# Band softmax sums split by key halves, band groups normalized in other steps, and other issue orders in a transformer layer on one core

## The chip, the cores and the metric

The kernel runs on one core of a Trainium2 chip. The metric is device time in microseconds (us) of one execution; the time before is the median of three runs. The names of the profile are used: PE is TensorE's matrix products, PEld its weight loads, DVE VectorE, ACT ScalarE, POOL GpSimd, SP SyncE, which issues most of the DMAs.

## The reference

One transformer layer on x of shape (2, 256, 128, 128), that is batch, time T, bands FB, channels C, in float32. Three residual blocks follow each other:

```
xt = LN(x);  x = x + MHA(xt over T,  4 heads, causal mask)
xf = LN(x);  x = x + MHA(xf over FB, 4 heads, mask |i - j| <= 16)
xn = LN(x);  x = x + (gelu(xn @ w1.T + b1) @ w2.T + b2)      # inner width 512
```

MHA is softmax(q k^T / sqrt(32) + mask) v with input and output projections. The attention over bands works on 128 positions, and each query sees the keys at most 16 positions away.

## The kernel before, in words

**Groups and runs.** The work is cut into groups of four tiles of 128 positions by 128 channels (512 columns). 128 groups of attention over time (`OverTime`) come first. Then come 16 runs; a run is 8 groups of attention over bands (`OverBands`, here "band groups", numbered 0 to 7) and then the 8 groups of the feed-forward block (`FeedForward`) on the same data. The first of the 16 runs overlaps the end of the attention over time.

**Steps.** `BoundedPath.run` (L1275 on) writes out the order of everything by hand. Step n of its loop works on several groups at once: the scores, exponentials and masks of group n, the weighing of group n-1, the output product of group n-2, queries, keys and values of group n+1, the fetch of the normalized input of group n+2, the normalization of group n+3, and statistics further ahead. Each engine runs its instructions in the order in which they are written (`InOrder`, L897 to L909, pins them; for this reason nearly every instruction of the profile carries line L907). An instruction that has to wait therefore holds up everything behind it on its engine.

**Products.** `product` (L646) makes a product of 128 by 128 by N as four, one for each strip of 32 output partitions, so that four tiles of the array of 128 rows by 32 columns (`128*32` in the profile) work side by side. The scores use tiles of 32 by 64 (`32*64`), eight side by side. Every float32 product shows as two instructions.

**One step of a band group, n.** On PE, in this order: the scores of n (L775; heads 0 to 3, for each tile two halves of 64 keys by 80 queries); the sums of the softmax weights of n-1 (L814, the product of ones with the weights p, `128*32`, 512 columns a head, into the bank `rp`); the weights times the values (into `op`); the output product of n-2 (L630); queries and keys of n+1 (L571), then values (L590). On ACT: four exponentials of the scores, Ln and Exp that invert the sums of n-1 (L602), the copies of queries, keys and values. On POOL: the band masks of heads 0 to 2, two instructions each (L800); head 3 is masked on DVE ahead of its exponential (L790). On DVE: the mask of head 3, the normalization and the 32 by 32 transposes of group n+3 (L441 and L458), the add of the output product of n-2 (L636), then the division for n-1 (L615: rp times r0, then u, then oT), then in some steps the statistics of a feed-forward group (L1302). The transposed tiles go through DRAM: `turn` writes them with four DMAs, `fetch` reads them one step later.

**Roots.** The reciprocal root of a group's variance is taken on POOL (`root`). For the first three feed-forward groups of a run the statistics are written in band steps 3, 4 and 5, behind the division, and the root at the head of steps 4, 5 and 6, ahead of that step's masks in POOL's order.

**A feed-forward step.** On PE: the first two of four hidden blocks of n (L841), the second product of n-1 (L869, four column tiles, four accumulated parts each), the last two hidden blocks of n. On ACT: GELUs, two and two. On DVE: normalization of n+3, the add of the second product (L886), statistics. After each second add four DMAs on SP store the result.

**Banks.** PSUM has eight banks of 512 columns. Outside the attention over time they were handed out in turn (L943), whoever asked next.

Of the kernel before, what the change touches and what calls it, by code (L numbers as in the profile page):

```python
# [19 lines left out]
P = 128  # L20
H = 4
D = 32
# [12 lines left out]
LARGE = 1e20  # L35
EXP_SET = "natural_log_exp_and_others"
# [327 lines left out]

def by_tile(t):

    return t.rearrange("p (i t q) -> p i t q", i=NT, q=D)


class Group:  # L370
# [7 lines left out]
    def __init__(self, path, src, dst, before=None, store=None):  # L378
        self.path, self.src, self.dst = path, src, dst
        self.before, self.store = before, store  # L380

# [76 lines left out]
    def turn(self):  # L458
# [3 lines left out]
        z = path.work.tile([P, H, P], F32, name="z", bufs=2)  # L462
# [98 lines left out]
class Attention(Group):  # L561
    which = None
    swapped = ()
# [7 lines left out]
    def queries_keys(self):  # L571
        path = self.path
        wf = path.k.wf[self.which]
        self.qp = path.bank([P, NT * P], "qp", self.place.get("qp", path.held.pop("qp", None)))
        product(path, self.qp, wf[:, 0:P], self.xnT)

        self.kp = path.bank([P, NT * P], "kp", self.place.get("kp"))
        product(path, self.kp, wf[:, P : 2 * P], self.xnT)

    def take_query(self):  # L580
        path = self.path
        self.qT = path.work.tile([P, NT * P], F32, name="qT")
        path.scalar.activation(self.qT, self.qp, AF.Identity, bias=path.k.bq[self.which], scale=1.0)

    def take_key(self):
        path = self.path
        self.kT = path.work.tile([P, NT * P], F32, name="kT")
        path.scalar.copy(self.kT, self.kp)

    def values(self):  # L590
        path = self.path
        wv = path.k.wf[self.which][:, 2 * P : 3 * P]
        self.vp = path.bank([P, NT, P], "vp", self.place.get("vp"))
# [3 lines left out]
    def take_values(self):  # L597
        path = self.path
        self.v = path.work.tile([P, NT, P], F32, name="v", bufs=4)
        path.scalar.copy(self.v, self.vp)  # L600

# [13 lines left out]
    def divide(self):  # L615

        path, vector = self.path, self.path.vector
        if self.r0 is None:
# [3 lines left out]
            vector.tensor_scalar(self.oT, u, -1.0, None, ALU.mult)  # L622
            return
        vector.tensor_tensor(self.rp, self.rp, self.r0, ALU.mult)
# [3 lines left out]
        vector.tensor_tensor(by_rows(self.oT), by_tile(self.op), by_tile(u), ALU.mult)  # L628

    def output(self):  # L630
        path = self.path
        self.yp = path.bank([P, NT, P], "yp", self.place.get("yp", path.held.pop("yp", None)))
# [3 lines left out]
    def finish(self):  # L636
        self.path.vector.tensor_tensor(self.dst(), self.yp, self.dst(), ALU.add)
        if self.store is not None:
            self.store()
# [13 lines left out]
class OverTime(Attention):  # L653
# [7 lines left out]
    def values(self):  # L661
        path = self.path
        wv = path.k.wf[self.which][:, 2 * P : 3 * P]
        self.vp = [path.bank([P, 2, P], "vp", self.place.get(f"vp{s}")) for s in range(2)]
# [5 lines left out]
    def take_values(self):  # L670
        path = self.path
        self.v = path.work.tile([P, NT, P], F32, name="v", bufs=4)
        for s in range(2):
            path.scalar.copy(self.v[:, 2 * s : 2 * s + 2], self.vp[s])

    def first_tiles(self):
# [3 lines left out]
        self.s0 = {h: path.bank([P, 2, 2 * P], "sp", path.banks[f"a{h}"]) for h in range(H)}  # L680

    def second_tiles(self):
# [3 lines left out]
        self.s1 = {h: path.bank([P, 2, P], "sp", path.banks[f"b{h}"]) for h in range(H)}  # L686
# [15 lines left out]
    def first_weights(self, heads):  # L702
        for h in heads:
            self.path.scalar.activation(self.p0[:, :, h], self.s0[h], AF.Exp)

    def second_weights(self, heads):
        for h in heads:
            self.path.scalar.activation(self.p1[:, :, h, 0], self.s1[h], AF.Exp)

# [17 lines left out]
    def weigh(self):  # L727
        path, v = self.path, self.v
        rp = path.bank([P, 2, 2, P], "rp", self.place.get("rp"))
# [4 lines left out]
        op = path.bank([P, 2, 2 * P], "op", self.place.get("op"))  # L734
# [33 lines left out]
class OverBands(Attention):  # L768
# [3 lines left out]
    follow = ("yp",)  # L772
    by_vector = 1

    def scores(self, heads):  # L775
        path = self.path
        self.sp = {h: path.bank([P, NT * P], "sp") for h in heads}
# [12 lines left out]
    def first_function(self):  # L790
# [6 lines left out]
        for h in range(H):  # L797
            path.scalar.activation(self.p[:, h].rearrange("p i q -> p (i q)"), self.sp[h], AF.Exp)

# [13 lines left out]

    def weigh(self):  # L814
        path = self.path

        path.held = {name: path.turn_of_bank() for name in self.follow}
        self.rp = path.bank([P, NT * P], "rp")
        for h in range(H):
            path.tensor.matmul(  # L820
                self.rp[rows_of(h), :], path.k.ones[:, 0:D], self.p[:, h].rearrange("p i q -> p (i q)"),
                start=True, stop=True,
            )
        self.op = path.bank([P, NT * P], "op")
# [7 lines left out]
class FeedForward(Group):  # L832
    last = False
# [679 lines left out]
```

## Time and profile before

| | |
|---|---|
| timed runs | 2631.95, 2633.58 and 2634.81 us, median 2633.58 |
| span of the profiled execution | 2631.9 us, granted TensorE clock 1.000 |
| attention over time | up to about 920 us of the span |
| 16 runs of band and feed-forward groups | the rest, some 106 us each |
| DVE, ACT, POOL busy | 81%, 70%, 74% of the span |
| HBM read and written | 167.98 MB and 166.72 MB |

The profiled execution has a span of its own, from its first to its last instruction; the timed runs also hold what lies around it. Times in rows of a timeline are from the start of the span. A row of the timeline gives start, duration, engine, line, operation, output<-inputs, shapes and how many instructions were merged; in brackets the idle time of the engine ahead of it and what ended that. A row of a group gives busy time and the mean of one in ns, then idle time and who ended it.

### The profile page before, as it was taken

The page shows a single profiled execution, that of the slowest core. Times are in us where ns is not written, and L with a number is a line of the kernel's source. Part 1 is how long each engine was busy: PE and PEld are TensorE (multiplying, and loading weights), DVE is VectorE, ACT ScalarE, POOL GpSimd, SP SyncE. Part 2 cuts the span into 40 slices and gives each one's busy share as a digit, 9 for nine tenths or more (in the row PEclk, how much of TensorE's full clock was granted, in tenths as well). Part 3 has the DMA queues.
Part 4 walks back from the last instruction along what each step waited for, and adds up shares of the span by engine and source line. Part 5 has one row for each costly group of instructions (what it writes and reads, how often), then busy time and mean ns, then how long its engine had stood idle before and what let it go on. Part 6 is the DMA issues. An engine that isn't in the chain of part 4 may idle for free.

```text
span 2631.9 us, 156460 instructions
## 1 busy us (share of the span) xinstructions
PE 2617.8 (99%) x68688; PEld 1837.4 (70%) x68688; DVE 2140.8 (81%) x6410; ACT 1838.8 (70%) x3543; POOL 1958.6 (74%) x2311
## 2 busy tenths in 40 slices
PE   9999999999999999999999999999999999999999
PEld 6666666666766767666777776667676677777776
DVE  8888888888888887977878779788797797887974
ACT  7989988999899875564655746647557466475573
POOL 7999999999999987666667666665776666757762
PEclk9999999999999999999999999999999999999999
DMA  6656555565565454445454544554454445554543
GB/s 155 167 149 158 149 149 149 155 155 149 149 158 149 122 127 119 115 123 127 118 124 124 123 122 117 126 128 120 122 126 120 120 119 131 123 120 123 123 104 88
DMA packets 469797, 344.97 MB, mean 131 GB/s; under 512 B 43120, under 2 KB 404464, under 8 KB 469104
## 3 DMA queue, kind: packets, MB, share of 16 engines
q1 hardware_dynamic: 468408, 334.41, 50.5%
q8 instruction: 540, 8.85, 1.5%
q14 instruction: 153, 1.25, 0.2%
q10 hardware_dynamic: 696, 0.46, 0.1%
HBM read 167.98 MB, written 166.72 MB: 127 GB/s over the span
## 4 chain that ended last, share of the span: by engine, by line
PE 99%; DVE 0%; issue 0%; DMA 0%; ACT 0%; ACTq 0%; DVEq 0%
PE bank L907 99%; DMA x<-in_x 0%; DVE xh L907 0%; DVE bank L907 0%; DVE res L907 0%; DVE stats L907 0%; DVE oT L907 0%; DVE u L907 0%; DVE xnT L907 0%; ACTq L907 0%; ACT p L907 0%; DVE vy L907 0%; ACT lnv L907 0%; DVE mv L907 0%; ACT root L907 0%
## 5 line engine op out<-in xcount | busy, mean ns | idle before, releaser
L907 ACT ACTIVATE hT<-bank,b 128x512 f32<-128x512 f32 x512 | 348.1, 688 | 524.2 <-PE bank L907 483.2
L907 POOL TENSOR_SCALAR_AFFINE_SELECT pf<-pf 128x512 f32<-128x512 f32 x768 | 477.7, 637 | 185.3 <-ACT pf L907 159.1
L907 PEld LDWEIGHTS bank<-w2T_sb,hT 128*32 128x32 f32 x16384 | 467.4, 110 | 54.8 <-issue 29.0
L907 PE MATMUL bank<-xnT,wf 128*32 128x512 f32 x4096 | 492.4, 592 | 0.5 <-DVE xnT L907 0.5
L907 PE MATMUL bank<-xnT,w1f 128*32 128x512 f32 x4096 | 486.3, 592 | 0.2 <-issue 0.2
L907 PE MATMUL bank<-w2T_sb,hT 128*32 128x128 f32 x16384 | 482.8, 273 | 1.0 <-issue 1.0
L907 ACT ACTIVATE p<-bank 128x512 f32<-128x512 f32 (+1 forms) x1024 | 430.6, 494 | 62.9 <-PE bank L907 62.9
L907 DVE TENSOR_SCALAR xh<-x,mv,rstd 128x160 f32<-128x160 f32 (+1 forms) x1012 | 394.3, 432 | 59.7 <-POOL rstd L907 49.4
L907 POOL TENSOR_SCALAR_AFFINE_SELECT p<-p 128x1024 f32<-128x1024 f32 (+2 forms) x384 | 364.5, 949 | 57.5 <-ACT p L907 49.1
L907 PEld LDWEIGHTS bank<-wf,xnT 128*32 128x32 f32 x8192 | 243.3, 110 | 144.1 <-issue 101.6
L907 POOL TENSOR_TENSOR p<-p,p 128x512 f32<-128x512 f32 x256 | 324.6, 1291 | 10.6
L907 DVE BATCH_NORM_STATS2 stats<-x 128x6 f32<-128x128 f32 x1536 | 329.0, 276 | 3.4 <-DMA x<-in_x 3.4
L907 POOL TENSOR_SCALAR rstd<-mv 128x4 f32<-128x4 f32 x251 | 57.8, 230 | 361.7 <-DVE mv L907 360.5
L907 PEld LDWEIGHTS bank<-xnT,w1f 128*32 128x32 f32 x4096 | 183.6, 110 | 171.6 <-issue 109.6
L907 PE MATMUL bank<-qT,kT 32*64 32x80 f32 (+4 forms) x16384 | 302.0, 271 | 0.1
L907 PEld LDWEIGHTS bank<-qT,kT 32*64 32x64 f32 x16384 | 260.0, 131 | 51.2 <-ACT kT L907 50.6
L907 DVE TENSOR_TENSOR res<-bank,res 128x512 f32<-128x512 f32 (+1 forms) x259 | 170.3, 658 | 153.3 <-PE bank L907 144.7
L907 ACT ACTIVATE pf<-bank 128x512 f32<-128x512 f32 x512 | 265.8, 602 | 35.5 <-PE bank L907 31.3
L907 PE MATMUL bank<-wn,oT 128*32 128x128 f32 x8192 | 283.8, 274 | 0.1
L907 DVE STREAM_TRANSPOSE z<-xh 128x512 f32<-128x512 f32 x380 | 270.3, 711 | 13.3
L907 PE MATMUL bank<-wf,xnT 128*32 128x128 f32 x8192 | 276.5, 273 | 0.0
L907 POOL TENSOR_TENSOR rstd<-rstd,mhalf 128x4 f32<-128x4 f32 x251 | 260.8, 1039 | 20.9
(100 smaller groups left out, 3820.3 us busy)
## 6 DMA issues: line engine op xcount, KB each, us to landing
turned<-z SPq DMA_DIRECT2D x1520, 64.0 KB, 2.7
xnT<-turned SPq DMA_DIRECT2D x380, 256.0 KB, 3.2
x<-res SPq DMA_DIRECT2D x256, 128.0 KB, 2.5
x<-x SPq DMA_DIRECT2D x128, 256.0 KB, 4.1
out<-res SPq DMA_DIRECT2D x252, 128.0 KB, 2.3
x<-in_x SPq DMA_DIRECT2D x124, 256.0 KB, 4.3
x<-in_x SPq DMA_DIRECT2D x4, 128.0 KB, 2.8
x<-in_x SPq DMA_DIRECT2D x6, 64.0 KB, 2.9
```

Of the source, the lines that this page charges most:

```text
L907: return self.tc.keep_in_program_order(emit(*args, **kwargs))
```

## The change

Four things are changed in the runs; the attention over time keeps its order.

1. *Sums in two parts*, for band groups 0 to 6 of each run (those whose next group is a band group too). The queries 0 to 47 of a tile see only the keys 0 to 63, and the queries 80 to 127 only the keys 64 to 127. Their sums are products over 64 keys, one half into `rp`, the other into a bank of its own, `lower`; the 32 queries in the middle are summed over 128 keys. The outer sums come directly behind the scores. Ln and the multiplication by r0 are made in two parts each.
2. *Orders in band steps.* The queries of n+1 are computed (and their copy queued) between the outer and the middle sums, ahead of the output product; keys and values stay where they were.
3. *Orders in feed-forward steps.* The second product of n-1 is split after two column tiles, with the third hidden block of n between the halves. The stores are put one step later, from ScalarE's queue in feed-forward steps.
4. *Normalization ahead.* When group n+3 is a band group (not of the first run), band group n+6 is normalized and turned in the same step. So groups 3 to 7 are done three steps earlier: groups 3, 4 and 5 in the last three feed-forward steps of the run before, 6 and 7 in band steps 0 and 1, and band steps 2, 3 and 4 normalize nothing. The tiles in DRAM get 8 buffers for 3, z gets 3 for 2.

Banks are now taken from a list of free ones in the order in which their last readers were written.

```diff
+EDGE = HALF - BAND
...
+    def outer_sums(self):
+
+        self.split = True
+        self.rp = self.take("rp", [P, NT * P])
+        self.lower = self.take("lower", [P, NT * EDGE])
+        for h in range(H):
+            self.sums_of(h, in_tiles(self.rp)[:, :, 0:EDGE], slice(0, EDGE), slice(0, HALF))
+            self.sums_of(h, in_tiles(self.lower), slice(P - EDGE, P), slice(HALF, P))
+
+    def middle_sums(self):
+        q = slice(EDGE, P - EDGE)
+        for h in range(H):
+            self.sums_of(h, in_tiles(self.rp)[:, :, q], q, slice(0, P))
+
+    def sums_of(self, h, to, q, rows):
+        self.path.tensor.matmul(
+            to[rows_of(h)], self.path.k.ones[rows, 0:D], self.p[rows, h, :, q],
+            start=True, stop=True, skip_group_check=True,
+        )
+
+    def invert(self):
...
+        path.scalar.activation(in_tiles(ln)[:, :, 0 : P - EDGE], in_tiles(self.rp)[:, :, 0 : P - EDGE], AF.Ln)
+        path.scalar.activation(in_tiles(ln)[:, :, P - EDGE : P], in_tiles(self.lower), AF.Ln)
+        self.r0 = path.work.tile([P, NT * P], F32, name="r0", bufs=2)
+        path.scalar.activation(self.r0, ln, AF.Exp, scale=-1.0)
+
+    def multiply(self):
...
+        vector.tensor_tensor(rp[:, :, low], in_tiles(self.lower), r0[:, :, low], ALU.mult)
+        self.give("lower")
+        vector.tensor_tensor(rp[:, :, q], rp[:, :, q], r0[:, :, q], ALU.mult)
...
     def weigh(self):
         path = self.path
 
-        path.held = {name: path.turn_of_bank() for name in self.follow}
-        self.rp = path.bank([P, NT * P], "rp")
-        for h in range(H):
...
+        if self.split:
+            self.middle_sums()
+        else:
+            self.rp = self.take("rp", [P, NT * P])
...
-        self.op = path.bank([P, NT * P], "op")
+        self.op = self.take("op", [P, NT * P])
...
+    def weigh_around(self, other):
+
+        self.zp = self.take("zp", [P, NT, P])
+        self.weigh_tiles(range(0, 2))
+        other.hidden((2,))
+        self.weigh_tiles(range(2, NT))
+        other.hidden((3,))
...
+        def turn_ahead(n):
+            for i in (n + 3, n + 6):
+                ahead = at(n + 3, OverBands) and at(i, OverBands) and i not in run0
+                if not at(i, OverTime) and (i == n + 3 or ahead) and not at_turn(i):
+                    do(i, "normalize", "turn")
...
+            self.storing = self.scalar if feeds[2] and n < len(groups) - NT else self.sync
+            do_at(n - 2, FeedForward, "put")
...
-            do_at(n + 3, (OverBands, FeedForward), "normalize", "turn")
+            turn_ahead(n)
...
-            do(n - 1, "weigh")
+            if bands[1] and bands[2]:
+                do(n - 1, "outer_sums")
+            if bands[2] and bands[3]:
+                do(n + 1, "queries")
+            if feeds[1] and feeds[2]:
+                groups[n - 1].weigh_around(groups[n])
+            else:
+                do(n - 1, "weigh")
             do(n - 1, "invert_exactly" if turn else "invert")
+            if bands[2] and bands[3]:
+                do(n + 1, "take_query")
...
             if bands[2] or turn:
                 do(n - 2, "output", "finish")
...
             do(n - 1, "divide")
...
             if bands[2] or turn:
                 statistics_of_feed(n)
-            if not turn:
+            if feeds[1] and feeds[2]:
+                do(n, "second_function")
+            elif not turn:
                 do(n, "second_half", "second_function")
...
-            do_at(n + 1, OverBands, "queries_keys", "take_query", "take_key")
+            if bands[2] and bands[3]:
+                do(n + 1, "keys", "take_key")
+            else:
+                do_at(n + 1, OverBands, "queries_keys", "take_query", "take_key")
```

In the code `bands[i]` and `feeds[i]` say whether group n-2+i is a band group or a feed-forward group, and `turn` marks the first feed-forward step behind a band step.

More of the change, by code (lines that the diff above doesn't have):

```diff
@@ L380, in __init__, with take, give @@
         self.before, self.store = before, store
+        self.taken = {}
+    def take(self, name, shape, i=None):
+        free = self.path.free
+        if i is None:
+            i = free[0]
+        if i in free:
+            free.remove(i)
+        self.taken[name] = i
+        return self.path.bank(shape, name, i)
+    def give(self, *names):
+        for name in names:
+            if name in self.taken:
+                self.path.release(self.taken.pop(name))
     def load(self):
@@ L562 @@
     which = None
+    split = False
+    keep = False
     swapped = ()
```

128 lines of the change are left out of this document (90 added, 38 removed).

## The prediction

> **What bounds the kernel now.** I read the page first: busy shares and the chain that ended last.
>
> ```profile
> span 2631.9 us, 156460 instructions
> PE 2617.8 (99%) x68688; PEld 1837.4 (70%) x68688; DVE 2140.8 (81%) x6410; ACT 1838.8 (70%) x3543; POOL 1958.6 (74%) x2311
> PE 99%; DVE 0%; issue 0%; DMA 0%; ACT 0%; ACTq 0%; DVEq 0%
> ```
>
> TensorE is never visibly idle, so only work taken off it, or waits that hide inside its busy time, can move the end. Next the timeline of TensorE over one step of a band group (step 3 of a run of eight band groups, counted from 0):
>
> ```profile
> 1266.30 0.97 PE L907 MATMUL bank<-qT,kT 32*64 32x80 f32 x64
> 1267.20 1.06 PE L907 MATMUL bank<-pf,ones 128*32 128x512 f32 x8
> 1268.08 1.06 PE L907 MATMUL bank<-pf,v 128*32 128x128 f32 x32
> 1268.95 1.06 PE L907 MATMUL bank<-wn,oT 128*32 128x128 f32 x32
> 1269.83 1.90 PE L907 MATMUL bank<-xnT,wf 128*32 128x512 f32 x16
> 1271.55 1.06 PE L907 MATMUL bank<-wf,xnT 128*32 128x128 f32 x32
> 1272.53 0.97 PE L907 MATMUL bank<-qT,kT 32*64 32x80 f32 x64
> ```
>
> From start to start: scores 0.90, sums 0.88, values weighed 0.87, output product 0.87, queries and keys 1.72, values 0.98; the step is 6.23. Every float32 product is two instructions. A block of 32 with 128 columns takes 0.87 (27 ns each) where the next block has the same tile shape, and 0.98 where the next has another (`128*32`, then `32*64`): a change of tile shape costs about 0.11.
>
> What feeds the sums is the other half. Step 3's chain on VectorE (normalization of a later group, then the add of the output product, division, statistics of the first feed-forward group), then on GpSimd:
>
> ```profile
> 1268.06 1.60 DVE L907 TENSOR_SCALAR xh<-x,mv,rstd 128x160 f32<-128x160 f32 x4
> 1269.70 0.71 DVE L907 STREAM_TRANSPOSE z<-xh 128x512 f32<-128x512 f32 x1
> 1270.34 0.65 DVE L907 TENSOR_TENSOR x<-bank,x 128x512 f32<-128x512 f32 x1
> 1270.91 0.69 DVE L907 TENSOR_TENSOR bank<-bank,r 128x512 f32<-128x512 f32 x1
> 1271.64 0.69 DVE L907 SCALAR_TENSOR_TENSOR u<-bank,r 128x512 f32<-128x512 f32 x1
> 1272.36 0.69 DVE L907 TENSOR_TENSOR oT<-bank,u 128x512 f32<-128x512 f32 x1
> 1272.97 0.86 DVE L907 BATCH_NORM_STATS2 stats<-x 128x6 f32<-128x128 f32 x4
> 1273.75 0.36 DVE L907 BATCH_NORM_AGGREGATE mv<-stats 128x2 f32<-128x6 f32 x4
> ...
> 1274.20 0.23 POOL L907 TENSOR_SCALAR rstd<-mv 128x4 f32<-128x4 f32 x1 [2.28 <-DVE mv L907]
> 1274.51 1.04 POOL L907 TENSOR_TENSOR rstd<-rstd,mhalf 128x4 f32<-128x4 f32 x1
> 1275.52 3.94 POOL L907 TENSOR_SCALAR_AFFINE_SELECT pf<-pf 128x512 f32<-128x512 f32 x6
> ```
>
> GpSimd sits 2.28 us until the statistics are there, takes the root, and only then masks step 4's weights, because the root stands first in its queue. The masks end at 1279.46; TensorE wants them for the sums in step 5. The next two rounds, and the sums that wait for each:
>
> ```profile
> 1276.88 0.65 DVE L907 TENSOR_TENSOR x<-bank,x 128x512 f32<-128x512 f32 x1
> 1283.42 0.65 DVE L907 TENSOR_TENSOR x<-bank,x 128x512 f32<-128x512 f32 x1
> ...
> 1282.07 3.94 POOL L907 TENSOR_SCALAR_AFFINE_SELECT pf<-pf 128x512 f32<-128x512 f32 x6
> 1288.61 3.94 POOL L907 TENSOR_SCALAR_AFFINE_SELECT pf<-pf 128x512 f32<-128x512 f32 x6
> ...
> 1279.65 1.07 PE L907 MATMUL bank<-pf,ones 128*32 128x512 f32 x8
> 1285.88 1.22 PE L907 MATMUL bank<-pf,ones 128*32 128x512 f32 x8
> 1292.27 1.38 PE L907 MATMUL bank<-pf,ones 128*32 128x512 f32 x8
> ```
>
> The masks end 0.19 before the first of these sums, 0.13 after the start of the second (1286.01 against 1285.88), 0.28 after that of the third. Those sums last 1.22 and 1.38 instead of 1.07: one head's column strip lags by 0.15 and 0.31 while the rest go on, and the lag is paid later. So in steps 3 to 7 a round of add, statistics, root, masks, sums runs almost exactly as long as two TensorE steps. That round decides my forecast.
>
> **The change, part by part.**
>
> *Sums in two parts* (7 of the 8 groups of each of 16 runs, 112 groups). Out: 8 instructions, 0.88. In: 16 of 64 rows by 192 columns, tile `64*32`, and 8 of 128 by 128 columns. No row shows `64*32`. A 512-column pass, four strips side by side, takes 0.88/2 = 0.43 without the shape change, so 192 columns take 0.16. The scores run eight tiles at once (64 instructions in 0.90, 14 ns each), so I let the eight outer tiles run together: two passes 0.32, first weights and stagger 0.06, one more change of shape 0.11, together 0.49. The middle: 8 x 27 ns = 0.22, and 0.02 for first weights moves to the next block. Sum 0.73 for 0.88: **0.15 less a group**, a step of 6.08. Bounds: 0.25 less if the added change is free, 0.15 more if the two key halves run one after the other (four passes, 0.64).
>
> The added change goes from `64*32` to `128*32`, a pair that no row here has. [...]
>
> *VectorE and ScalarE.* The multiply becomes two (192 and 320 columns), the logarithm two.
>
> ```profile
> L907 ACT ACTIVATE p<-bank 128x512 f32<-128x512 f32 x512 | 292.2, 597 | 0.6 <-PE bank L907 0.6
> L907 ACT ACTIVATE p<-bank 128x256 f32<-128x256 f32 x512 | 183.6, 390 | 62.3 <-PE bank L907 62.3
> L907 DVE TENSOR_TENSOR res<-bank,res 128x512 f32<-128x512 f32 x255 | 169.2, 663 | 149.6 <-PE bank L907 141.0 <-POOL pf L907 5.9 <-ACT p L907 2.6
> L907 DVE TENSOR_TENSOR res<-bank,res 128x128 f32<-128x128 f32 x4 | 1.1, 291 | 3.7 <-PE bank L907 3.7
> ```
>
> Fixed part of one: ScalarE 2 x 390 - 597 = 0.18; VectorE 291 - 372/3 = 0.17. Independent neighbours overlap (the add starts 0.57 before the multiply although it lasts 0.65), so I take +0.13 on VectorE and, as the second logarithm starts under the first, +0.03 on ScalarE's chain (bounds 0 and 0.18).
>
> *Queries moved ahead of the weighing.* This helps ScalarE (its query copy no longer sits behind TensorE), but pushes the output product back: it starts at 0.90 + 0.49 + 0.88 + 0.22 + 0.87 = 3.36 into the step, not 2.65. It also needs its input 2.1 sooner than the old 1269.83 (3.53 into the step): 1.39. The fetch is issued a step earlier and lands 3.2 later:
>
> ```profile
> 1275.15 0.34 SPq L907 DMA_DIRECT2D xnT<-turned  x1
> xnT<-turned SPq DMA_DIRECT2D x380, 256.0 KB, 3.2
> ```
>
> This one would be there at 1278.35, due at 1278.76 + 1.39 = 1280.15: hidden by 1.8, and steps 2 to 4 put no transposes' DMAs ahead of it any more. A late one would cost what it is late.
>
> *Normalization elsewhere.* Steps 2 to 4 lose the four normalizations and the transpose, 2.3 us of VectorE each. In the old step 3 these set the add: product ready at 1268.95 + 1.06 + 0.06 = 1270.07, add at 1270.34, 4.04 into the step. Now the add waits for the product alone: 3.36 + 1.12 = **4.48, later by 0.44**. VectorE idles ahead of it, and nothing queued behind may pass. So the relief buys nothing for the round. Step 0, which weighs a feed-forward group, keeps its blocks. The steps that take the work have room:
>
> ```profile
> 1349.22 0.69 DVE L907 TENSOR_TENSOR res<-bank,res 128x512 f32<-128x512 f32 x1 [2.94 <-PE bank L907]
> 1349.98 0.69 ACT L907 ACTIVATE hT<-bank,b 128x512 f32<-128x512 f32 x1 [3.66 <-PE bank L907]
> L907 ACTq DMA_DIRECT2D out<-res x2: 552/924/1295, 2624.5 to 2626.2; - x2
> ```
>
> In a feed-forward step VectorE idles 2.94 before its add, more than the 2.3 that three steps a run take on; the four more DMAs stand on SyncE's queue behind that step's fetch, and the tiles they write are fetched only three to five steps later. ScalarE idles 3.66: four stores at the mean of its only two such issues, 0.92, are 3.7 in every second step, between two pairs of GELUs that have a TensorE block of 1.72 to spare. I cost both at nothing; at 1.3 a store the late GELUs would hold up TensorE by 0.5, three times a run, +24 in all: the bound. Two column tiles of the feed-forward product ahead of the third hidden block change the order of one tile shape: nothing.
>
> *Where the 0.15 arrives.* Step 1 has no output product and is shorter:
>
> ```profile
> 1361.13 0.97 PE L907 MATMUL bank<-qT,kT 32*64 32x80 f32 x64
> 1365.84 0.58 ACT L907 COPY kT<-bank 128x512 f32<-128x512 f32 x1
> 1366.49 0.78 PE L907 MATMUL bank<-qT,kT 32*64 32x80 f32 x43
> ```
>
> The scores begin 0.07 after the copy of the keys, the last of a gapless ScalarE chain. TensorE would be there 0.15 sooner, the copy 0.03 later: step 1 saves nothing (-0.15 + 0.17). Steps 2 to 7 save 0.15 each on TensorE, but in steps 3 to 7 the round decides. New round from the start of step n: add 4.48; to the end of the statistics (1273.75 + 0.36, 7.81 into the old step 3) 7.81 - 4.04 + 0.13 = 3.90, so 8.38; the masks (old end 1279.46, 13.16) end 13.16 - 7.81 = 5.35 later, 13.73; with the 0.03 that the old lags show beyond the mask's end, 13.76. The sums of step n+2 are due at 2 x 6.08 + 0.90 = 13.06. **They wait 0.70.** The change of tile shape right behind the outer sums lets no strip run ahead, so all of TensorE waits. It happens in step 5; step 5 is then 0.70 longer, so the round from step 4 fits; the one from step 5 makes step 7 wait 0.70 again.
>
> A run: 7 x -0.15, +0.17 in step 1, 2 x +0.70, and the old lags of 0.15 and 0.31 go: -1.05 + 0.17 + 1.40 - 0.46 = +0.06. Fifteen runs: +0.9. The first run keeps its normalizations in place, its VectorE falls behind and its three rounds wait some 0.7 each (an estimate from the same rows), +0.5 in all. Together +1.4 on the span of 2631.9. The timed runs, 2631.95 to 2634.81, contain what lies around the span; I add to their median, 2633.58: **2635 us**, no change that can be told (a measurement here tells about 0.2%, 5.3 us). An error of 0.1 in the outer sums enters about four times a run (step 2, two rounds, step 7): 6.4 us; so the forecast's own range is 2628 to 2643.
>
> **Rivals.**
>
> *The round does not bind* (faster). For it: VectorE has 2.3 us less in steps 2 to 4, and the old round missed by only 0.13 and 0.28. Against: the add follows the product, which moved back, and the statistics stay behind the division. Then a run gives -1.05 + 0.17 - 0.46 = -1.34, sixteen runs -21: **2612**.
>
> *The outer halves run one after the other* (slower). For it: no row has `64*32`, and the two halves of a head write the same partitions. Against: the scores' eight tiles, and a bank of its own for the lower half. Outer 0.79 instead of 0.49: step 1 +0.15, step 2, the two rounds and step 7 +0.30 each, 1.35 a run, with the +0.09 from above +1.44, sixteen runs +23: **2658**. From an outer part of about 0.57 it would be measurably slower.
>
> *Issue bound* (slower): 24 small instructions for 8. The 64 scores go out at 14 ns each, so 16 more cost at most 0.22 beyond what the array hides, 112 x 0.22 = 25: 2660, if nothing hid them; but 0.49 for 16 is 31 ns each, twice that pace. [...]
>
> **Chances.** Forecast 0.55; the round does not bind 0.24; halves in turn 0.13; issue bound 0.02; stores on ScalarE hold up GELUs, 0.06. The forecast's 0.55 I split by its range: faster 0.10, same 0.39, slower 0.06. Faster 0.24 + 0.10 = 0.34; same 0.39 + 0.01 (the stores, little) = 0.40; slower 0.06 + 0.13 + 0.02 + 0.05 = 0.26. The range, 2606 to 2648, takes in the first rival, a free change of shape with it in part, and the stores' lower half; the halves in turn and what lies beyond are left out, some 2 in 10.
>
> **What would show it.** A block of outer sums of 0.49 and a middle of 0.22 in TensorE's timeline; 0.79 means halves in turn, 0.39 a free change of shape. An add 4.5 into step 3 with idle time before it that ends by TensorE; masks ending 13.7 after the start of step 3; outer sums in steps 5 and 7 (not 6) with some 0.7 of idle or stretched time by GpSimd. Scores of step 2 waiting for ScalarE's key copy. I am wrong if steps 3 to 7 all take 6.1, or if the feed-forward steps grow longer.

## The result, and the profile after

The changed kernel takes **2675.57 us** (median of five runs, 2672.97 to 2677.6) for 2633.58: a ratio of 1.0157, 95% interval 1.0145 to 1.0169. It is slower by 42 us; the prediction was 2635, range 2606 to 2648. The spans of the two profiled executions, 2674.7 and 2631.9 us, differ as much, so the traces can be set against each other. In the table of experiments below, the times of e1 and e16 leave out one much slower execution each (7461 and 4477 us); with it the median of e1 is 2647.84, from which later expectations start.

The page of after, busy shares and the chain that ended last:

```profile
span 2674.7 us, 160410 instructions
PE 2633.1 (98%) x70480; PEld 1792.1 (67%) x70480; DVE 2161.9 (81%) x6522; ACT 1836.4 (69%) x3655; POOL 1960.3 (73%) x2311
PE 76%; DVE 15%; DMA 2%; POOL 2%; ACT 2%; issue 2%; SPq 1%; ACTq 0%; DVEq 0%; POOLq 0%
```

Before, the chain was TensorE from end to end. Now VectorE and GpSimd stand in it, and so does "issue": time in which TensorE waited for nothing that the profile shows. The waits of TensorE, before and then after (us in all, times, longest):

```profile
PE bank L907 <- issue: 4.4, 9, 1.3
```

```profile
PE bank L1020 <- issue: 14.6, 23, 2.1
PE bank L1020 <- POOL pf L1020: 6.4, 23, 0.7
PE bank L1020 <- DVE ok L1020: 4.6, 1, 4.6
PE bank L1020 <- DVE oT L1020: 2.5, 14, 0.2
```

These sum to less than 42: a stall of one column strip stretches a block and shows only in part as idle time (in step 3 of run 4 below, 0.16 us of idle time stand for a step that is 0.74 longer). The loss is better read from one row of scores to the next. First the blocks, in TensorE's timeline of after (run 3, steps 2 and 3):

```profile
1272.00 0.97 PE L1020 MATMUL bank<-qT,kT 32*64 32x80 f32 x64
1272.90 0.56 PE L1020 MATMUL bank<-pf,ones 64*32 64x192 f32 x16
1273.38 1.06 PE L1020 MATMUL bank<-xnT,wf 128*32 128x512 f32 x8
1274.27 0.40 PE L1020 MATMUL bank<-pf,ones 128*32 128x128 f32 x8
1274.48 1.06 PE L1020 MATMUL bank<-pf,v 128*32 128x128 f32 x32
1275.36 1.06 PE L1020 MATMUL bank<-wn,oT 128*32 128x128 f32 x32
...
1278.08 1.04 PE L1020 MATMUL bank<-qT,kT 32*64 32x80 f32 x64
...
1281.51 0.62 PE L1020 MATMUL bank<-wn,oT 128*32 128x128 f32 x16
1282.78 0.65 PE L1020 MATMUL bank<-wn,oT 128*32 128x128 f32 x16 [0.66 <-issue]
```

The outer sums take 0.48 and the middle 0.21, and step 2 takes 6.08: the sizes of the prediction. In step 3 TensorE stops for 0.66 between the 16th and the 17th matmul of an output product, which nothing but issue releases. Run 4 shows the whole loss. The steps are differences between starts of score rows (the last entry is step 7 with the feed-forward steps); the unstalled values are the shortest that recur in after and in the experiments below:

| run 4 | step 0 | 1 | 2 | 3 | 4 | 5 | 6 | 7 and feed-forward | sum |
|---|---|---|---|---|---|---|---|---|---|
| after | 7.12 | 5.40 | 6.07 | 6.81 | 6.12 | 6.90 | 6.11 | 62.72 | 107.26 |
| after, unstalled | 7.12 | 5.40 | 6.07 | 6.07 | 6.07 | 6.07 | 6.07 | 61.47 | 104.34 |

Step 3 loses 0.74 where a wait by issue stands, the only one in it. Steps 5 and 7 lose 0.83 and some 0.86 to the masks. Their rows (scores and the late matmul of step 3, then step 5, then the first feed-forward step; below, GpSimd's masks for step 5):

```profile
1386.36 0.97 PE L1020 MATMUL bank<-qT,kT 32*64 32x80 f32 x64
...
1388.95 0.59 PE L1020 MATMUL bank<-xnT,wf 128*32 128x512 f32 x1 [0.16 <-issue]
...
1400.18 0.59 PE L1020 MATMUL bank<-pf,ones 64*32 64x192 f32 x8
1401.03 0.53 PE L1020 MATMUL bank<-pf,ones 64*32 64x192 f32 x8 [0.26 <-POOL pf L1020]
...
1429.86 0.41 PE L1020 MATMUL bank<-wn,oT 128*32 128x128 f32 x6 [0.18 <-DVE oT L1020]
```

```profile
1395.71 0.23 POOL L1020 TENSOR_SCALAR rstd<-mv 128x4 f32<-128x4 f32 x1 [3.74 <-DVE mv L1020]
1396.02 1.04 POOL L1020 TENSOR_TENSOR rstd<-rstd,mhalf 128x4 f32<-128x4 f32 x1
1397.04 3.94 POOL L1020 TENSOR_SCALAR_AFFINE_SELECT pf<-pf 128x512 f32<-128x512 f32 x6
```

GpSimd sits 3.74 us until the statistics are there and masks from 1397.04 to 1400.98, and the sums due at 1400.18 wait. In the first feed-forward step the output product of the last band group also waits for its division (oT). Over the 16 runs: runs 1 to 14 take 108.42 on average for 106.09 (14 x 2.33 = 33), run 0 takes 116.75 for 107.88 (9), run 15 and the start 1: together the 43 us between the spans.

**Theory A**: the round of add, division, statistics, root and masks is late, as the prediction had it. **Theory B**: TensorE's instructions come late. The trace supports B in one more way. The page lists a queue of kind "instruction":

```profile
q8 instruction: 555, 9.09, 1.5%
```

By the count it carries TensorE's instructions: 555 packets of 16,384 bytes, and TensorE has 141,646 recorded instructions (2 x 70,480 matmuls and weight loads, the rest mostly waits on semaphores), 255 a packet; full packets of 256 would hold 142,080. The kernel before has 540 packets for 137,886 recorded instructions, 255 a packet again. In after the first packet lands 15.3 us into the span and the last at 2674.0 of 2674.7 us, so they come in during the whole execution. I counted all of them in order of start. All 27 idle times over 0.1 us that end by issue after 930 us have their first instruction at count 194 or 195 modulo 256, and it starts 1.27 to 1.69 us after a packet has landed:

```
  start us   idle ns  count    mod 256   last packet landed
  1282.78       658   68290      194        -1.47
  1495.68      1115   79555      195        -1.32
  1614.25      1224   85954      194        -1.27
  1929.55      1335  102595      195        -1.33
  2257.20      2117  120002      194        -1.40
```

The kernel before has nine such idle times behind 930 us, at the same two counts, 1.25 to 1.51 us after a packet has landed. A band step used to have 368 matmuls and weight loads in 6.23 us, 256 in 4.33. It now has 400 in 6.07, 256 in 3.89.

### The profile page after: what moved, and what is told of

Same layout as the page of the kernel before. It is cut to its first block, busy times and chain, and to the rows that moved or that the text cites. A ratio compares the mean times of both kernels' runs of the same rounds, so it can differ in the third digit from the quotient of the medians.

```text
span 2674.7 us, 160410 instructions
## 1 busy us (share of the span) xinstructions
PE 2633.1 (98%) x70480; PEld 1792.1 (67%) x70480; DVE 2161.9 (81%) x6522; ACT 1836.4 (69%) x3655; POOL 1960.3 (73%) x2311
## 3 DMA queue, kind: packets, MB, share of 16 engines
q14 instruction: 155, 1.27, 0.2%
## 4 chain that ended last, share of the span: by engine, by line
PE 76%; DVE 15%; DMA 2%; POOL 2%; ACT 2%; issue 2%; SPq 1%; ACTq 0%; DVEq 0%; POOLq 0%
PE bank L1020 76%; DVE xh L1020 3%; DVE bank L1020 2%; DVE ln L1020 2%; DVE u L1020 2%; DVE x L1020 2%; DVE oT L1020 2%; DVE stats L1020 2%; DVE z L1020 1%; DMA xnT<-turned 1%; POOL rstd L1020 1%; DMA turned<-z 1%; POOL pf L1020 1%; ACT pf L1020 1%; SPq L1020 1%
## 5 line engine op out<-in xcount | busy, mean ns | idle before, releaser
L1020 PEld LDWEIGHTS bank<-w2T_sb,hT 128*32 128x32 f32 x16384 | 459.0, 110 | 147.1 <-issue 121.6
L1020 PE MATMUL bank<-xnT,wf 128*32 128x512 f32 x4096 | 517.7, 595 | 2.3 <-DMA xnT<-turned 1.0
L1020 PE MATMUL bank<-xnT,w1f 128*32 128x512 f32 x4096 | 492.1, 594 | 4.6 <-DVE ok L1020 4.6
L1020 PE MATMUL bank<-w2T_sb,hT 128*32 128x128 f32 x16384 | 495.0, 273 | 1.3 <-ACT hT L1020 0.8
L1020 PE MATMUL bank<-qT,kT 32*64 32x80 f32 (+4 forms) x16384 | 307.7, 272 | 8.1 <-issue 6.4
L1020 PEld LDWEIGHTS bank<-qT,kT 32*64 32x64 f32 x16384 | 263.2, 131 | 62.7 <-ACT kT L1020 52.0
L1020 DVE TENSOR_TENSOR bank<-bank,r 128x192 f32<-128x192 f32 (+1 forms) x352 | 185.4, 527 | 107.5 <-PE bank L1020 79.9
L1020 PEld LDWEIGHTS bank<-wn,oT 128*32 128x32 f32 x8192 | 220.9, 110 | 35.5 <-DVE oT L1020 17.0
```

The source lines that it names most:

```text
L1020: return self.tc.keep_in_program_order(emit(*args, **kwargs))
```

## The experiments

All are made from the changed kernel unless said otherwise. Times are medians; the ratio is to the kernel before on the same chip; "issue" is TensorE's idle time ended by issue in the profiled execution (4.4 before, 14.6 after).

| run | statistics first | split | also | us | ratio, 95% interval | issue |
|---|---|---|---|---|---|---|
| e1 | yes | all | | 2646.93 | 1.0023 to 1.0053 | 20.4 |
| e2 | no | none | | 2648.34 | 1.0040 to 1.0074 | 3.4 |
| e3 | no | all | old normalization | 2677.92 | 1.0139 to 1.0173 | 14.6 |
| e4 | no | all | old feed-forward order, stores at once on ScalarE | 2806.13 | 1.0631 to 1.0666 | 15.4 |
| e5 | yes | all | loads moved | 2640.46 | 1.0001 to 1.0032 | 4.5 |
| e6 | no | none | sums in pieces, head after head | 2798.25 | 1.0593 to 1.0629 | 0.9 |
| e7 | no | all | all orders old | 2660.91 | 1.0076 to 1.0109 | 18.9 |
| e8 | yes | all | old feed-forward order and stores | 2645.22 | 1.0010 to 1.0049 | 16.8 |
| e9 | yes | all | wide scores | 2637.58 | 1.0006 to 1.0025 | 1.0 |
| e10 | no | none | sums in pieces, heads in turn | 2678.39 | 1.0150 to 1.0184 | 18.7 |
| e11 | kernel before | none | wide scores | 2648.22 | 1.0048 to 1.0081 | 0.4 |
| e12 | yes | all | loads, verdict's bank, wide scores | 2637.51 | 1.0009 to 1.0028 | 1.1 |
| e13 | yes | none | verdict's bank | 2629.86 | 0.9976 to 0.9994 | 1.7 |
| e14 | yes | steps 2 to 4 | loads, verdict's bank | 2629.17 | 0.9972 to 0.9992 | 3.4 |
| e15 | yes | all | loads, verdict's bank | 2634.24 | 0.9991 to 1.0009 | 6.4 |
| e16 | yes | none | loads, verdict's bank | 2628.26 | 0.9966 to 0.9985 | 1.9 |

**e1, the statistics first.** `statistics_of_feed` of a band step is called ahead of the sums, so that VectorE does it before the add:

```diff
-            if not bands[2] and not turn:
+            if not turn:
                 statistics_of_feed(n)
...
-            if bands[2] or turn:
+            if turn:
                 statistics_of_feed(n)
```

> The changed kernel (2675.6 us) with the statistics of the first feed-forward groups moved ahead of the output product's add on VectorE, in band steps. Theory A (the round of add, division, statistics, root and masks holds up TensorE in steps 5 and 7, some 1.4 us a run in 15 runs, more in the first): the root is on time, the masks end early, the waits of the outer sums for GpSimd go, 2650 to 2655 us. Theory B (the rest is TensorE's instruction fetch, whose stalls come because blocks of 256 instructions are used up faster): stalls by issue, 14.8 us after 940 us, stay or grow by some us, so not under 2645. Rival (the wait for the masks only covers another one): 2668 or more, idle time of TensorE of the same sum with another releaser.

2646.93: 28.6 us of the 42 are gone, somewhat more than expected (2650 to 2655). GpSimd's timeline in e1 and TensorE's waits after 940 us:

```profile
1381.75 0.23 POOL L1020 TENSOR_SCALAR rstd<-mv 128x4 f32<-128x4 f32 x1
1382.06 1.04 POOL L1020 TENSOR_TENSOR rstd<-rstd,mhalf 128x4 f32<-128x4 f32 x1
1384.89 3.94 POOL L1020 TENSOR_SCALAR_AFFINE_SELECT pf<-pf 128x512 f32<-128x512 f32 x6 [1.79 <-ACT pf L1020]
```

```profile
PE bank L1020 <- issue: 19.9, 27, 1.6
PE bank L1020 <- DVE ok L1020: 2.5, 1, 2.5
```

The root no longer waits, the masks follow the exponentials, and both waits for GpSimd and for oT are gone. The part of step 7 and the feed-forward steps, 62.7 in most runs of after, is 61.5 or less in seven of runs 1 to 14. Theory A holds. Its size is smaller than the 28.6: some 5 us of them are a shorter wait in the first run (2.5 us for 4.6, and without the stretch at half the granted clock that follows it in after; see e13). Theory B is untouched: the stalls by issue grew.

**e2, without the outer sums; e10 and e6, without them but with as many instructions.** e2 drops the call of `outer_sums`, and `weigh` makes the sums as before. e10 makes the same sums in 128-column pieces, and e6 the same pieces in the other order:

```diff
-            for h in range(H):
-                path.tensor.matmul(self.rp[rows_of(h), :], ...)
+            for i in range(NT):
+                for h in range(H):
+                    path.tensor.matmul(self.rp[rows_of(h), c], ..., self.p[:, h, i], ...)
```

> The changed kernel without the outer sums: the sums of all 512 columns in one part behind the queries, everything else as changed. Theory B (density of TensorE's instructions, 400 in 6.07 us for 368 in 6.23 us, makes the fetch stalls): stalls by issue fall from 14.8 us to about 3, as before the change. Theory A: the sums are due 0.88 later behind the queries, so the masks are on time and 1.4 us a run go. The split itself gives back 0.15 x 7 x 16 = 17. Sum 2675.6 + 17 - 21 - 12 = 2660, with less in the first run still 2655. Rival (the stalls come of the transfers that bunch up in other steps): stalls stay at 14 us, 2672.

> The kernel without the split (2648.3 us, stalls by issue 3.4 us), its sums cut into four of 128 columns, now the four heads in turn, so that the strips work side by side: the same products and tile shape in 0.88, 416 instructions in a step for 368. Theory B: 12 us of stalls or more, 2657 to 2665. Rival (the stalls belong to the 64-row tiles or to their change of shape): stalls 3 to 4 us, 2648.

> The kernel without the split (2648.3 us, stalls by issue 3.4 us), its sums of 512 columns cut into four of 128: the same products and tile shape, 416 instructions of TensorE in a step for 368. Theory B (the number of instructions in a stretch makes the stalls): 12 us of stalls or more, 2657 to 2665. Rival (the stalls belong to the 64-row tiles or to the change of tile shape): stalls stay at 3 to 4 us, 2648.

e2 ended 7 to 12 us under what A and B gave together: the sum had taken the split's stalls at their idle time, and they cost more. The step from e2 to e10 is the plainest test of B. No tile shape or data transfer changes, and the same sums are made; only the instructions in a band step go from 368 to 416. The stalls by issue go from 3.4 to 18.7 us and the time up by 30, 13 us beyond what B expected. The step without a stall is 6.24 for 6.23, so the 30 us are not the price of the smaller products; up to 5 of them come from the granted clock, which is 0.50 for 13.6 us of e10 and for 3.4 of e2. e10's waits after 940 us:

```profile
PE bank L1022 <- issue: 18.7, 26, 2.3
PE bank L1022 <- DVE ok L1022: 4.3, 1, 4.3
PE bank L1022 <- POOL pf L1022: 1.4, 5, 0.4
```

All the idle times by issue again begin at 194 or 195 modulo 256. e6 was meant as this test and missed its time: with the pieces head after head, four matmuls in a row go to one strip, and the strips no longer work side by side. The block's rows by form, e6 and then e10 (128 groups, so 2.44 us a group for 1.14; the step is 7.62 for 6.24):

```profile
L1022 PE MATMUL bank<-pf,ones 128*32 128x128 f32 x4096 | 312.3, 275 | 0.0
```

```profile
L1022 PE MATMUL bank<-pf,ones 128*32 128x128 f32 x4096 | 146.0, 274 | 2.1 <-POOL pf L1022 1.4
```

So e6 is a control instead: the same 416 instructions are spread over 7.62 us, 256 in 4.69, and its stalls by issue are 0.9 us in all. It is the pace that makes them, and not the number or the size of the pieces.

**e9, e11 and e12, fewer instructions.** The scores of a head and tile in one product of 32 by 128, also outside the band: 336 instructions in a split band step for 400, and 304 for 368 in the kernel before (e11).

```diff
-            for e in range(2):
...
+            q = slice(i * P, (i + 1) * P)
+            for h in heads:
+                path.tensor.matmul(self.sp[h][:, q], self.kT[r, q], self.qT[r, q], start=True, stop=True)
```

> The kernel with the statistics first (2647.8 us, stalls by issue 20.2 us) with the scores of a head and tile in one product of 32 by 128 over 128 queries in place of two of 32 by 64 over 80: also the scores outside the band are computed, and masked like before. TensorE has 336 instructions in a band step for 400, in the same time if four such tiles run side by side (8 x 0.109 = 0.87 for 0.90). Theory B (the number of instructions in a stretch makes the stalls): stalls 4 us or less, 2627 to 2633. Rival (density does not decide): stalls 15 to 20, 2645. If the tiles run one after the other: a score block of 1.7 or more, 2740.

> The kernel before the change (2635 us) with the scores in products of 32 by 128 over 128 queries: 304 instructions in a band step for 368. Theory B: its own stalls, some 3 to 4 us, go, and 0.03 a step with them: 2626 to 2631. Rival: 2635.

> The changed kernel with the statistics first, the loads moved out of band steps 1 to 6, the wide scores, and the bank of the verdict's product put at the end of the list of free banks (the first feed-forward steps wait 2.5 to 4.6 us for it). If theories A and B hold all that was lost: 16 runs near 104.3 us for 105.7 to 106, 2612 to 2620. If a rest of the loss is elsewhere: 2625 or more.

The stalls go, as B expected: in e9 runs 1 to 14 all take 106.05 us, one of them 106.12, where e1's lay between 105.35 and 108.76. But the score block was mis-estimated. TensorE's timeline of e9:

```profile
1375.56 1.17 PE L1014 MATMUL bank<-qT,kT 32*128 32x128 f32 x32
1376.66 0.56 PE L1014 MATMUL bank<-pf,ones 64*32 64x192 f32 x16
```

1.10 from start to start, not 0.87: 0.20 more a step than the 0.90 of the narrow scores, which eats what the stalls gave back. About 0.11 of the miss, by an estimate from the 0.98 for 0.87 of the values' block before, is the change of tile shape behind the block, which the 0.87 left out. 106.05 less eight times 0.21 is 104.4, the unstalled run of the table above (6.28 is the step for 6.07), so the change's own saving is there once nothing stalls. All three missed their times by that block: e12 less 128 times 0.20 would be 2612.

**e3, the old normalization; e5, the loads moved.** e3 normalizes group n+3 only. e5 is e1 with the loads of the next run's input issued in steps 7 to 11 in place of 2 to 9:

```diff
-            for i in (n + 3, n + 6):
+            for i in (n + 3,):
```

```diff
-                do(i, "load")
+                if not at(i, OverBands) or i in run0:
+                    do(i, "load")
+            for j in {7: (16, 17), 8: (18, 19), 9: (20,), 10: (21, 22), 11: (23,)}.get(...):
```

> The changed kernel with every band group normalized at its old step (n+3 only). Theory A: VectorE gets 2.3 us of work back in steps 2 to 4, but the add still waits for the product, so the round stays: 2672 to 2680. Theory B by density: the stalls by issue in step 3 stay at some 14 us. Rival (the stalls are those of fetches that collide with input loads and transposes moved to other steps): stalls fall to 3 us, 2663.

> The kernel with the statistics first (2647.8 us), and the loads of the next run's input taken from band steps 2 to 6 to step 7 and the first four feed-forward steps. Theory B1 (TensorE's instructions come late where a dense stretch meets many transfers: in the run with the old normalization the stalls had the same sum but lay in steps 2 to 7, not in step 3): stalls by issue fall from 20.2 us to 8 or less, step 3 comes down to 6.1, 2635 us. Rival B2 (density alone decides, transfers only place the stalls): stalls 15 to 20 us, 2645 to 2649.

e3 changes nothing in the time. The idle time by issue keeps its sum but not its place: of after's 14.8 us behind 930 us (idle times from 0.1 us on), 10.5 lie in band step 3; of e3's 14.8 us only 1.2 do, and nearly all the rest in steps 2 and 4 to 7. That is not what B by density alone had expected, some 14 in step 3 as before. The queue of SyncE in after shows what stands in steps 2 and 3 (run 4):

```profile
1381.09 0.38 SPq L1020 DMA_DIRECT2D xnT<-turned  x1
1381.57 1.75 SPq L1020 DMA_DIRECT2D x<-x  x1
1383.41 0.44 SPq L1020 DMA_DIRECT2D xnT<-turned  x1
1383.91 0.43 SPq L1020 DMA_DIRECT2D x<-x  x1
1386.48 0.34 SPq L1020 DMA_DIRECT2D xnT<-turned  x1
1386.88 1.08 SPq L1020 DMA_DIRECT2D x<-x  x1
```

With no transposes to wait for, SyncE runs ahead and issues six transfers of 256 KB in 6 us. In e5 the loads are gone from there and the stalls by issue fall from 20.4 to 4.5, though the time misses B1's 2635 by 5. So in these runs density makes the stalls, and how many there are and where changes with the transfers beside it. The gain in time, 6.5 us at the medians, is less sure: e5's ten runs spread from 2629.48 to 2646.78.

**e7, e8 and e4, the orders.** e7 has the split and the free list of banks with every order as before; e8 is e1 with the old feed-forward order and SyncE's stores. e4 is e8 without the statistics first, and its stores stay on ScalarE's queue, a step earlier; its expectation took them to be on SyncE's.

> The split with the list of free banks alone: queries, normalization, feed-forward order and stores as before the change. Theory A: without the queries ahead the output product starts 0.88 sooner, the add is bound by the normalization as before, so the outer sums wait some 0.3 twice a run, not 0.7. A and B: 15 runs x (-1.05 + 0.17 - 0.46 + 0.6) = -11 us, stalls by issue +11, so 2630 to 2640. Rival (most of the loss is the bank list's or the split's own): 2650 or more.

> The kernel with the statistics first (2647.8 us) with the old order of the feed-forward steps and its stores on SyncE's queue at once. If the new order and ScalarE's stores cost nothing, as the prediction had it: 2645 to 2650, feed-forward part of a run 61.5 us. If they cost what the feed-forward steps grew by: 2640 or less. If they gain: over 2652.

> The changed kernel with the old order of the feed-forward steps and the stores at once on SyncE's queue. Theory A and B: the feed-forward steps lose only what their own order costs, at most the 0.36 us in the turn step and some fetch stalls, 2667 to 2675. Rival (stores on ScalarE hold up GELUs): 2650 to 2660, feed-forward part of a run from 62.75 to 61.9 us.

e8 against e1: 2645.22 and 2646.93, with intervals that overlap; 2645 to 2650 was expected if the order costs nothing. The new feed-forward order and its stores cost nothing that can be told, as the prediction had it. e7 was expected at 2630 to 2640 and is 25 us slower than before with the split alone, with 18.9 us of issue and only 2.1 us of waits for the masks: that is the number of its rival (most of the loss is the bank list's or the split's own). The list is not it, for e13 and e16 below have the list and are faster than the kernel before. If the stalls of the split make up the loss, they cost about twice what shows as idle, which the sum had not allowed for. e4 shows what the later place of the stores avoids. Put at once, they wait on ScalarE for the add, and the GELUs behind them wait too (ScalarE's timeline of e4); the feed-forward part grows to 71 to 73 us a run. The waits for GELUs sum to 94.5 us. With each of the 16 long ones, 3.9 to 5.8 us, the granted clock falls to 0.50 for 3.4 or 6.8 us; TensorE works through 70 us of that, so up to 35 us of the loss are the clock's. The row of one wait:

```profile
1606.17 1.98 ACTq L1020 DMA_DIRECT2D out<-res  x4
1608.20 2.42 ACT L1020 ACTIVATE hT<-bank,b 128x512 f32<-128x512 f32 x4 [5.66 <-DMA out<-res]
```

**e13 to e16, what is left.** e2 left 13 us unexplained. In after, TensorE also waits 4.62 us in the first run, behind the product of the verdict (the test that decides whether the other form of the softmax has to be run):

```profile
1018.85 0.39 PE L1020 MATMUL bank<-tests,ones 128*128 128x6 f32 x2
1023.85 3.64 PE L1020 MATMUL bank<-xnT,w1f 128*32 128x512 f32 x16 [4.62 <-DVE ok L1020]
1027.26 2.98 PE L1020 MATMUL bank<-w2T_sb,hT 128*32 128x128 f32 x64
```

The wait costs more than itself. From 1022.6 to 1029.4 us the granted clock of after is 0.50 (the last but two of the figures in this row of stretches):

```profile
1022.60:1029.40 6.80, 5.55 (x57) 2.76 (x61) 5.87 (x24) 1.38 (x2) 3.75 (x4) 0.50 0.57 135
```

The 16 products behind the wait take 3.41 from start to start, where the kernel before takes 1.74, and the next 64 take 2.81 for 1.75: 2.7 us more. In e1, with a wait of 2.5 us there, the clock does not fall.

The verdict's bank is the first of the free list and stays first, so the next block takes it at once and waits for the reader. The edit puts the bank at the list's end:

```diff
-        tp = self.bank([P, 6], "tp", self.free[0])
+        i = self.free[0]
+        tp = self.bank([P, 6], "tp", i)
+        self.release(i)
```

> The changed kernel without the split, with the statistics first and the verdict's bank at the end of the list. Without the split alone it was 2648.3 us, 13 more than before the change, with 3.4 us of stalls: that rest is open. Theory A (the rest is the round too, in the feed-forward part of 62.4 us for 61.6, and the verdict's wait of 4 us in the first run): a run 105.3 us for 106.0, the first run 4 less, 2620 to 2628. Rival (the bank list, the queries ahead or the normalization ahead cost the rest): 2635 or more.

> As the run with the statistics first and the loads moved, verdict's bank at the end of the list, but the sums split only for the groups weighed in band steps 2, 3 and 4, where no transposes are issued. Theory B with a threshold (dense stretches of three steps are carried by what has been fetched ahead): three times 0.16 a run under the kernel without the split, stalls by issue under 5 us: 2612 to 2625. Rival (any split step stalls by more than it gains): slower than the kernel without the split by 5 us or more.

> The statistics first, the loads moved, the verdict's bank at the end of the list, split in all seven groups: 2640.5 less the verdict's 3 us, 2634 to 2640. Stalls by issue 4 to 12 us.

> As e13 with the loads moved out of band steps 2 to 6. Theory B: at 368 instructions in 6.23 us few stalls are left to remove: 0 to 4 us faster than e13. Rival (the moved loads disturb the feed-forward part): slower than e13.

e13 is at 2629.86, so e2's rest was the round in the feed-forward part (62.41 for 61.63 us) and the verdict's bank. It is 1.9 over the upper end that theory A gave, and under the 2635 of the rival that the bank list or the moved queries and normalization cost the rest. e16 at 2628.26 is 6.5 us faster than the kernel before (ratio 0.9975), the fastest version here, and it has no split at all. With the same loads, e14 splits three groups a run and is not told apart from it; it misses the 2612 to 2625 that a threshold of density gave, and no run shows such a threshold. e15 splits seven and is 6 us slower, where the split should give some 14 (0.9 a run). The dense stretch never paid. e15 is e5 with only the verdict's bank moved: 2634.24 for 2640.46, where 3 us were expected; e5's spread is too wide to size it by that.

## Why the prediction was wrong

What held, by its own steps. The sizes: outer sums 0.48 (0.49 predicted), middle 0.21 (0.22), step 6.07 (6.08), step 1 at 5.40 (5.38), the add 4.55 into step 2 of run 3 (4.48); the halves do not run in turn. No row gave the 0.06 that the prediction puts between the end of a product and its add; 4.55 says 0.13. No run of before shows the change from `64*32` to `128*32`, which the sum priced at the 0.11 of other pairs. After shows it: at all 112 split groups the first `128*32` matmul starts 0.07 us before the last outer one ends, as at the other changes of shape; the weights times the values start 0.18 or more before the end of sums of their own shape. By these ends, which the profile models, the pair costs 0.11 too, and no strip runs ahead over it. A free change would have given 0.39 for the outer sums. The round: waits in steps 5 and 7, not 6, of 0.83 and some 0.86 for the 0.70 predicted (run 4; over all runs 24 of the 26 idle times over 0.1 us lie in steps 5 and 7). Undoing it gave 28.6 us, some 24 without the first run's shorter wait; the prediction's own two rows, 2612 without the waits and 2635 with them, are 23 apart. The stores, the feed-forward order and the moved normalization, priced at nothing, cost nothing that can be told. The saving of an unstalled run is 105.70 - 104.34 = 1.36; the rival "the round does not bind" had 1.34.

**The step that failed is the rival "Issue bound".** The sum put nothing for the pace of TensorE's instructions, and the rival said that 16 more small instructions "cost at most 0.22 beyond what the array hides", and dismissed even that because 31 ns each is twice the pace of the scores. That compares the instructions with the pace at which TensorE starts the scores, 14 ns each. What ran short was their supply: 16 matmuls and as many weight loads more in a step, a packet of 256 used up in 3.89 us for 4.33, and no stall of after ended sooner than 1.27 us after a packet had landed. "TensorE is never visibly idle" was a misreading: the kernel before had 4.4 us of idle time by issue in nine pieces, and its page lists the instruction queue. I read 0% in the chain and asked no further. The rival got 2 in 100; that its price of 25 us was about right is luck, since it did not name this reason. With the statistics first, the split costs 15 us net where it should give 14: 29 us, the larger part of the 41 by which the forecast was off.

Two smaller terms were mis-sized. The first run, priced at +0.5, took 8.9 more, of which 4.6 is the verdict's wait and 2.7 the half clock behind it. The bank list was described in the change but no reader that comes late was looked for. And in the feed-forward part the round has a third wait that the sum left out: the turn step's output product waits for oT. Of run 4's 62.72, the unstalled 61.47 and 0.86 for step 7's masks leave 0.39 for it. The prediction's own sign of being wrong, feed-forward steps that grow longer, was there: 62.7 for 61.9 in this part of a run. (Its 2658 for halves in turn is a slip: the terms beside it give 2657.)

Step by step, from the kernel before to the changed one: the other edits with both cures -5 (e13 against before), the split on top of them 14.6 (e1 less its 2.5, against e13), the verdict's bank 2.5 (its wait in e1), the late statistics 28.6 (after against e1; some 5 of it is the verdict's wait again, longer and with the clock at half). They give 41 of the 42 by the way these differences are taken, each from where the last one ends; the sum is no proof, and that a share has the cause it is named for rests on the traces above. The runs are of several chips, on which the kernel before takes 2633.4 to 2635.5.

What stays open: why in after a packet of instructions starts 0.2 us into a block of 256 in one place and 2.4 us in another. That moved loads reduce the stalls points to the transfers beside it; the wait of a packet ahead of its start was not measured by itself.

## What to carry to other kernels

Before a block is cut into more and smaller instructions, count the engine's instructions per microsecond over the whole stretch and look for idle time by issue in the kernel as it is: TensorE showed some of it here already (4.4 us, at 256 instructions in 4.33 us), and at 256 in 3.89 a saving in array time was no saving. Where a chain of short operations on two engines is nearly as long as the step that needs it, move the link that depends on nothing late (here the statistics) ahead of the one that does. A work list that hands out banks by order of release must be told of every reader, also of the one that runs once.

## What was not expected of the hardware

- The 555 packets of 16,384 bytes of after, one for 255 of TensorE's recorded instructions, landed during the whole execution, and the stalls by issue ended 1.27 to 1.69 us after one had landed (1.21 to 1.68 in e10).
- Time lost this way showed only in part as idle time: e10 has 15 us more of it than e2 and takes 30 us longer, of which up to 5 are the clock's.
- The granted clock fell to 0.50 for 3.4 or 6.8 us at some idle times of TensorE: in after at the verdict's 4.62 us and at a stall by issue of 2.12, in e4 at all 16 waits of 3.9 to 5.8; not at the 2.13 of e7 nor at the 2.47 of e1.
- 32 matmuls of 128 columns on four 32 by 128 tiles took 1.10 in e9, and on four 128 by 32 tiles 0.98 before, both with a change of tile shape behind them (34 and 31 ns each).
- The same 16 products of sums, four to a strip, took 2.44 us a group with the four of a strip in a row and 1.14 with the strips in turn (busy time, e6 and e10).
